# Dealing the second batch's selective scan out between the stages ahead of the first attention scores

## Chip, cores and metric

The kernel runs on one NeuronCore of a Trainium2 chip. The metric is device microseconds of that core for one launch; the figure for the kernel before is the median of 3 runs, 2120.05 us (2119.4 to 2121.59). A NeuronCore has TensorE (PE; its weight loads are shown apart as PEld), VectorE (DVE), ScalarE (ACT), GpSimd (POOL) and SyncE (SP), which issues the DMAs of this kernel.

## What is computed

The input x has 4 batches of 512 rows and 512 columns. Each batch goes through four residual blocks; each adds tanh of a gate times the block's result.

```
x += tanh(g0) * scan(ctx, z = layernorm(x))        # selective scan, 512 channels, 16 states
x += tanh(g1) * glu(layernorm(x))                  # ternary weights, 8-bit activations, 512 -> 2048 -> 512
x += tanh(g2) * attention(layernorm(x), ctx)       # 16 heads of 128, RMS-normed q and k
x += tanh(g3) * experts(layernorm(x))              # row t uses expert t % 4
scan: state = state * exp(delta * A) + (delta * u) * B ;  y = sum over 16 states of state * C
      y = (y + D * u) * silu(z)
glu:  out = bitlinear(silu(bitlinear(x, gate)) * bitlinear(x, val), out)
```

The batches are independent of one another; within a batch each block needs the one before it. The weights are scaled and split into float16 pairs (high and low part), so that three float16 matmuls stand for one of float32.

## The kernel before, in words

**Scan** (`scan(b)`, a generator). Four pieces of input projection and convolution (L507 to L523), four of softplus (L538 to L553), and then, twice over two channel tiles (`G=2`), 16 pieces, one for each state n, and four pieces that gate and add the result to x. A piece of a state loads two broadcast rows `bc` and `cc` (L590, L592), and for each of two channel tiles computes `dA` = exp on ACT (L596), `h` = du * bc on POOL (L186), the recurrence on DVE (L603, or L606 for 2 of 8), the product with `cc` on DVE (L604) or POOL, and four transposing matmuls that add the result up in PSUM (`py`, L579). A scan of this form is 48 pieces.

**GLU** (`bitnet(b)`, a generator of 24 pieces). Four row tiles; for each, the quantised rows (L669, L671), a DMA transpose (L673), four column blocks of gate and value matmuls (`pg` L687, `pv` L698) with their DVE steps (L692, L708, L710, L711), and the output projection (`po`, L733), whose operand passes through another DMA transpose (L731).

**Attention** goes head by head, in three phases that are one head apart: queries, scores with softmax, weighted sum. The main loop (from L1215) steps through 64 heads; in each it makes ten moves, and after each move it takes one piece of whatever stands in the list `behind`. Into that list go the scan and GLU of the next batch: batch 1 is entered 12 heads ahead of its own first head (`LEADS`), batches 2 and 3 16 heads ahead. So the second batch's scan and GLU lie beside heads of the first batch's attention. Keys of each group of four heads are made in some moves of the loop as well.

**Prologue.** Ahead of the main loop stand, in program order: the first batch's scan with the ternary weights between its pieces (L1173), the second batch's context (L1181), the first batch's GLU (L1182), the scaling and splitting ("staging") of the attention weights of head group 0 (L1183), the keys of group 0 (L1187), and the values of all four groups, 16 chunks that are stored to DRAM (`first_values`, L1188). Groups 1 and 2 are staged at iterations -1 and 1 of the main loop with large tiles (`STAGE`), group 3 from iteration 3 in small pieces (`staging_small`) that are taken two at a time after a softmax (`FILL0`, `filler`).

**Who decides the order.** The program's calls give priorities; a list scheduler in the build then decides the order in which instructions stand on each engine, and which buffer of a pool a tile gets. Work that is ready can therefore move ahead of its place in the program. On each engine, the SP queue too, instructions then start in that fixed order.

**Shared tiles.** The pool `mid` has six buffers of tag `g` and six of tag `v`. The scan's `bc` and `cc` and the GLU's hidden blocks `g` all take tag `g`; the scan's `h` and the GLU's `gv` take tag `v`. The four hidden blocks of a row tile stay in their buffers until that row tile is projected.[...]

Of the kernel before, what the change touches and what calls it, by code (L numbers as in the profile page):

```python
# [29 lines left out]
F32 = mybir.dt.float32  # L30
F16 = mybir.dt.float16
# [9 lines left out]
P = 128  # L41
# [23 lines left out]


MIDS = {"g": 6, "v": 6, "t": 4, "q": 2, "n": 1, "x": 1, "y": 2}
STAGE = (-1, 1)
STAGE_SMALL = {3: 3}
FILL0 = 2  # L70
RATE_S = 1.0
RATE_B = 1.0
SRB = 1
SHB = 1
EARLY = 1
SIDE0 = 5
SIDE1 = 1
SIDEN = 16
# [30 lines left out]
LO_POOL = {(b, h, 1) for b in range(3) for h in range(9, 16)}  # L109
HL = 2  # L110
PRE = 1
LEADS = {1: 12, 2: 16, 3: 16}
LEAD_B = 6


# [1 line left out]
def flamingo_kernel(  # L117
# [19 lines left out]
    def psum(pool, name, tag="m", bufs=None):  # L137
        if tag == "a":
            role = name.rstrip("_0123456789")
            tag = ATAG.get(role, "m")  # L140
            bufs = ABUF[tag]
        kw = {} if bufs is None else {"bufs": bufs}
        return pool.tile([P, 512], F32, tag=tag, name=name, **kw)

    def ap(name):
        return psum(psa, name, "a")
# [3 lines left out]
    def bigt(shape, dtype, name):  # L150
        return big.tile(shape, dtype, tag="big", name=name)
# [58 lines left out]
    def pow2(sq, name, pool=const, tag=None, bufs=1):  # L210
# [10 lines left out]
        nc.vector.reciprocal(S[:, 1:2], S[:, 0:1])  # L221
        return S

    def total_pow2(tot, pool, name):

        n = tot.shape[1]
        ps = ap(f"frobps{name}") if pool is None else psum(pool, f"frobps{name}")
        nc.tensor.matmul(ps[:, :n], ones, tot, start=True, stop=True)
        if n == 1:
            return pow2(ps[:, 0:1], name)  # L230
        s = sm(1, "ftot", f"ftot{name}")
        nc.vector.tensor_reduce(s, ps[:, :n], AX.X, ALU.add)
        return pow2(s, name)

    def frobenius(w, junk, pool, name):

        tot = sm(1, "frob", f"frob{name}")
        nc.scalar.activation(junk, w, AF.Square, accum_out=tot)
        return total_pow2(tot, pool, name)
# [16 lines left out]
    wq_d, wk_d, wo_d = [], [], []  # L256
    Sq, Sk, Sv, So, ceq = [], [], [], [], []

    def raw_load(name, src):
        raw = bigt([P, src.shape[1] * src.shape[2]], F32, f"raw{name}")  # L260
        with tc.issue_after(pin[0]) if pin[0] and PINS else nullcontext():
            nc.sync.dma_start(raw.rearrange("p (a b) -> p a b", a=src.shape[1]), src)
        return raw
# [3 lines left out]
    def run(steps):  # L267
        while True:
            try:
                next(steps)  # L270
            except StopIteration as e:
                return e.value

    def staging(name, src, n, ps_pool, raw=None, store=True):

        if raw is None:
            raw = raw_load(name, src)
        w = raw.shape[1]
        hl = bigt([P, 2 * w], F16, f"hl{name}")
        v = hl.rearrange("p (n s m) -> p n s m", n=n, s=2)  # L280
        pieces = [
            (raw[:, j * 512 : (j + 1) * 512], *(v[:, j, s] if n > 1 else v[:, 0, s, j * 512 : (j + 1) * 512] for s in range(2)))
            for j in range(w // 512)
        ]
        tot = sm(4, "stot", f"stot{name}", 2)
        for j, (r, hi, lo) in enumerate(pieces):
            nc.scalar.activation(hi, r, AF.Square, accum_out=tot[:, j : j + 1])
            yield
        S = total_pow2(tot[:, : len(pieces)], ps_pool, name)
        for r, hi, lo in pieces:  # L290
            split(r, hi, lo, S[:, 1:2])
            yield
        if not store:
            return None, S, hl
        d = dram.tile([P, 2 * w], F16, name=f"d{name}")
        nc.sync.dma_start(d, hl)
        return d, S, hl
# [29 lines left out]
            yield  # L327
        return d, S, None

    def stage_attention_weights(hg, ps_pool):  # L330
        run(attention_weights(hg, ps_pool, staging))

    def attention_weights(hg, ps_pool, staging):
        cols = slice(hg * 512, (hg + 1) * 512)
        d, S, _ = yield from staging(f"wq{hg}", Wq[hg], HG, ps_pool)
# [26 lines left out]

    def first_values(pool, ps_tile):

        for hg in range(NG):
            raw = pool.tile([P, 2, 512], F32, tag="rv", name=f"rawv{hg}", bufs=2)
            nc.sync.dma_start(raw, Wv[:, hg * 512 : (hg + 1) * 512].rearrange("(k p) c -> p k c", p=P))
            wv = pool.tile([P, 2, 2, 512], F16, tag="wv", name=f"wv{hg}", bufs=2)
            S = frobenius(raw, wv[:, 0], psv, f"wv{hg}")
            split(raw, wv[:, 0], wv[:, 1], S[:, 1:2])  # L370
            Sv.append(S)
            wv_d.append(dram.tile([P, 2048], F16, name=f"dwv{hg}"))
            nc.sync.dma_start(wv_d[hg], wv.rearrange("p s k c -> p (s k c)"))
            for b in range(PRE):
                for c, v in enumerate(
                    values_of(b, hg, wv, ps_tile, lambda s, d, n: pool.tile(s, d, tag="v", name=f"o{n}", bufs=VB))
                ):
                    nc.sync.dma_start(v_d[b][hg][:, c, :], v.rearrange("p s c -> p (s c)"))


    gamma_w = const.tile([P, 3], F32, name="gamma_w")
# [65 lines left out]
    raw = bigt([P, 2, T * P], F32, "inpraw")  # L447
# [203 lines left out]
        nc.vector.tensor_scalar(dn, m, 1.0 / (127.0 * gain), None, ALU.mult)  # L651
        return up, dn

    def bitnet(b, w_tile=bigt, ps_tile=lambda name: psum(pss, name), biases=None):
        xt = x_sb[b]
        w3 = []
        for i in range(3):
# [20 lines left out]
        def hidden(t, xqT, sgv):  # L678

            nm = f"{b}{t}"  # L680
            hs = []
            mx = sm(4, "hmx", f"hmx{nm}")
            for n in range(4):
                cols = slice(n * 512, (n + 1) * 512)
                pg = psum(pss, f"pg{nm}{n}")
                for k in range(T):
                    nc.tensor.matmul(pg, xqT[:, k, :], wg[:, k, cols], start=k == 0, stop=k == T - 1)  # L687
                g = midt([P, 512], F32, f"g{nm}{n}", "g")
                if biases is None:
                    nc.sync.dma_start(g, gate_b[cols].partition_broadcast(P))  # L690
                gb = g if biases is None else biases[0][:, cols]
                nc.vector.scalar_tensor_tensor(g, pg, sgv[:, 0:1], gb, ALU.mult, ALU.add)  # L692

                th = pg
                nc.scalar.activation(th, g, AF.Tanh, scale=0.5)
                pv = ps_tile(f"pv{nm}{n}")
                for k in range(T):
                    nc.tensor.matmul(pv, xqT[:, k, :], wv[:, k, cols], start=k == 0, stop=k == T - 1)  # L698
                v = midt([P, 512], F32, f"gv{nm}{n}", "v")
                if biases is None:  # L700
                    nc.sync.dma_start(v, val_b[cols].partition_broadcast(P))
                vb = v if biases is None else biases[1][:, cols]
                if (b, n) in GVP:
                    v2 = midt([P, 512], F32, f"gv2{nm}{n}", "t")
                    nc.scalar.activation(v2, pv, AF.Copy, scale=sgv[:, 1:2])
                    nc.gpsimd.tensor_tensor(v, v2, vb, ALU.add)
                else:
                    nc.vector.scalar_tensor_tensor(v, pv, sgv[:, 1:2], vb, ALU.mult, ALU.add)  # L708
                pool_mult(g, g, v)
                nc.vector.scalar_tensor_tensor(g, th, 1.0, g, ALU.add, ALU.mult)  # L710
                nc.vector.tensor_reduce(mx[:, n : n + 1], g, AX.X, ALU.max, apply_absolute_value=True)  # L711
                hs.append(g)
                yield

            return hs, mx
# [413 lines left out]
    def filler(ins):  # L1129

        for _ in range(FILL if atts[B - 1] else FILL0):
            with tc.issue_after(ins):
                while fill and next(fill[0], fill) is fill:
                    fill.pop(0)

    ak = ctx.enter_context(tc.tile_pool(name="ak", bufs=1))
    with tc.tile_pool(name="pro", bufs=1) as pro, tc.tile_pool(name="psp", bufs=4, space=PSUM) as psp:

        psv = pss
# [39 lines left out]
            biases.append(wide([P, HID], F32, f"bias{name}"))  # L1179
            nc.sync.dma_start(biases[-1], bias.partition_broadcast(P))  # L1180
        context(1, wide, junk, psv)  # L1181
        run(bitnet(0, wide, lambda name: psum(psp, name, "n", 2), biases))  # L1182
        for hg in range(EARLY):  # L1183
            stage_attention_weights(hg, psv)
        atts[0] = step, keys = attention(0)
        steps[0] = step
        run(keys(0, lambda name: psum(psp, name, "m", 2)))  # L1187
        first_values(pro, lambda name: psum(psp, name, "m", 2))  # L1188
    psa = ctx.enter_context(tc.tile_pool(name="psa", bufs=4, space=PSUM))
    at_pool = ctx.enter_context(ExitStack())  # L1190
    at = at_pool.enter_context(tc.tile_pool(name="at", bufs=1))
# [6 lines left out]
            for t in range(T)  # L1198
        ]

    in_bitnet = [False]
    behind, rate = [], 0.0

    def layer0(b):

        in_bitnet[0] = False
        if b >= 2:
            context(b, bigt, bigt, pss)
        yield from scan(b)
        in_bitnet[0] = True  # L1210
        yield from bitnet(b)


    n = B * NH
    for i in range(-2, n):  # L1215
# [34 lines left out]
                        next(keygen, None)  # L1250
        if i in STAGE_SMALL:
            fill.append(attention_weights(STAGE_SMALL[i], None, staging_small))
        if i in STAGE:
            for hg, j in enumerate(STAGE):
                if j == i:
                    stage_attention_weights(hg + EARLY, pss)
        if i >= 0 and i % NH == NH - 1:
            finish(i // NH)
        if i == n - NH + STAGE_E:
# [73 lines left out]
```

## Time and profile before

| What | Value |
|---|---|
| median of 3 runs | 2120.05 us |
| the profiled execution's own time | 2116.47 us |
| its span, first to last instruction | 2114.7 us |
| mean granted TensorE clock | 0.864 |
| PE busy | 1619.9 us (77%) |
| DVE busy | 1659.6 us (78%) |
| ACT busy | 1202.2 us (57%) |
| POOL busy | 1006.5 us (48%) |

The page puts busy time against the span, splits the span into 40 slices, and lists the costliest groups of instructions with the idle time before them. Stage times below are taken from the trace: the first batch's scan writes `py` until 179 us; its GLU runs its matmuls from 203 to 294 us; the keys of group 0 are made from 289 to 305 us; the values of the first batch from 306 to 358 us; the first query matmul starts at 376.5 us; the second batch's scan writes `py` from 430 to 634 us and its GLU's matmuls run from 658 to 765 us. A window of the trace gives, for each engine, busy microseconds and number of instructions in a stretch of time, then the granted TensorE clock, the DMA engines' busy share and what they moved.

### The profile page before, as it was taken

To read this page: it belongs to the slowest core of one execution; us is meant where nothing else is said; L and a number is where in the kernel's file an instruction comes from. 1 tells how busy PE (TensorE), PEld (TensorE's weight loads), DVE (VectorE), ACT (ScalarE), POOL (GpSimd) and SP (SyncE) were. 2 spreads that over 40 slices of the span, in tenths; PEclk is the share of its full clock that TensorE was granted. 3 is DMA by queue.
4 is the path that set the end of the run, shared out by engine and by line. 5 is a ranking of instruction groups with operands and counts; after the bars stand their busy time and mean duration, and the time that the engine had idled before them with its cause. 6 is when DMAs were issued, how large, how long until landed. Compare 5 with 4: busy or idle time off the path is not lost. (4 is left out here: it accounts for less than half of the span.)

```text
span 2114.7 us, 26915 instructions
## 1 busy us (share of the span) xinstructions
PE 1619.9 (77%) x8238; PEld 905.6 (43%) x8238; DVE 1659.6 (78%) x3237; ACT 1202.2 (57%) x2575; POOL 1006.5 (48%) x914
## 2 busy tenths in 40 slices
PE   3464654777676988777898967787899879788986
PEld 1343221345443444454444434444444445445445
DVE  5798855699998987999998679998885665555753
ACT  6866355665544666564546664654465565657633
POOL 2775330276664545766536367774253431313211
PEclk8555867889888998888899988898999989899998
DMA  7454176667888866776776567767765776867753
GB/s 248 157 166 139 25 194 224 191 157 200 188 223 209 191 138 159 191 179 164 184 184 143 121 152 206 176 165 192 165 148 124 169 165 189 182 163 192 184 127 100
DMA packets 525202, 358.08 MB, mean 169 GB/s; under 512 B 424768, under 2 KB 427456, under 8 KB 519040
## 3 DMA queue, kind: packets, MB, share of 16 engines
q1 hardware_dynamic: 525056, 356.36, 66.9%
q8 instruction: 64, 1.05, 0.2%
q14 instruction: 82, 0.67, 0.1%
HBM read 214.98 MB, written 38.54 MB: 120 GB/s over the span
## 5 line engine op out<-in xcount | busy, mean ns | idle before, releaser
L186 POOL TENSOR_TENSOR h<-du,bc 128x512 f32<-128x512 f32 x256 | 333.5, 1322 | 88.1 <-PE py L579 69.5
L579 PE MATMUL py<-ident,h 128*128 128x128 f32 x1024 | 196.8, 339 | 118.8 <-DVE h L604 109.1
L596 ACT ACTIVATE dA<-delta,A 128x512 f32<-128x512 f32 x256 | 172.0, 687 | 191.5 <-DVE h L604 132.1
L902 ACT ACTIVATE pr<-ps,nmx,rqs 128x512 f32<-128x512 f32 x256 | 196.9, 774 | 124.2 <-DVE nmx L894 119.4
L603 DVE TENSOR_TENSOR_SCAN dA<-dA,h 128x512 f32<-128x512 f32 x208 | 249.3, 1216 | 11.6 <-ACT dA L596 11.3
L252 PE MATMUL ps<-kT,qT 128*128 128x512 f16 x768 | 214.4, 402 | 49.8 <-ACT pr L902 45.4
L252 PE MATMUL pq<-axnT,wq 128*128 128x512 f16 x768 | 213.5, 436 | 35.2 <-DMA axnT<-xsa 15.0
L252 PE MATMUL pav<-pT,v 128*128 128x256 f16 x1536 | 205.7, 286 | 43.6 <-DVE v L244 14.7
L579 PEld LDWEIGHTS py<-ident,h 128*128 128x128 f32 x1024 | 163.0, 213 | 161.3 <-DVE h L604 139.5
L926 DVE SCALAR_TENSOR_TENSOR hl<-pr,den,hl 128x512 f16<-128x512 f32 x214 | 195.8, 926 | 24.7 <-POOL hl L925 15.0
L252 PEld LDWEIGHTS <-v 128*128 128x128 f16 x1536 | 156.2, 103 | 99.1 <-issue 30.8
L884 DVE TENSOR_REDUCE nmx<-ps 128x1 f32<-128x512 f32 x256 | 172.7, 680 | 28.6 <-PE ps L252 27.9
L252 PE MATMUL pwo<-wo,oT 128*128 128x512 f16 x768 | 180.9, 384 | 9.9 <-DVE oT L244 5.2
L252 PEld LDWEIGHTS <-cT 128*128 128x128 f16 x768 | 83.7, 110 | 170.1 <-issue 108.8
L925 POOL TENSOR_SCALAR hl<-pr,den 128x512 f16<-128x512 f32 x86 | 64.5, 750 | 189.1 <-DVE den L912 59.7
L252 PEld LDWEIGHTS <-wq 128*128 128x128 f16 x768 | 85.0, 112 | 154.4 <-issue 92.4
L252 PE MATMUL pk<-wk,cT 128*128 128x512 f16 x384 | 119.1, 457 | 33.9 <-DVE ssq L873 11.3
L186 POOL TENSOR_TENSOR g<-g,gv 128x512 f32<-128x512 f32 x64 | 83.5, 1310 | 120.3 <-DVE gv L708 44.6
L252 PEld LDWEIGHTS <-qT 128*128 128x128 f16 x768 | 77.9, 103 | 143.7 <-issue 77.5
L604 DVE TENSOR_TENSOR h<-dA,cc 128x512 f32<-128x512 f32 x208 | 138.0, 676 | 0.6
L183 POOL TENSOR_TENSOR rqs<-ssq,mhalf 128x4 f32<-128x4 f32 x64 | 69.0, 1078 | 134.9 <-DVE ssq L873 101.5
L252 PE MATMUL pw<-wv,cT 128*128 128x512 f16 x384 | 102.5, 413 | 28.7 <-DVE ov L244 11.9
(379 smaller groups left out, 3442.0 us busy)
## 6 DMA issues: line engine op xcount, KB each, us to landing
bc<-bd SPq DMA_DIRECT2D x112, 256.0 KB, 3.9
cc<-bd SPq DMA_DIRECT2D x112, 256.0 KB, 4.3
wq<-dwq SPq DMA_DIRECT2D x64, 256.0 KB, 3.6
wo<-dwo SPq DMA_DIRECT2D x64, 256.0 KB, 4.0
w<-w3d SPq DMA_DIRECT2D x12, 1024.0 KB, 7.0
g<-in_gate_b SPq DMA_DIRECT2D x48, 256.0 KB, 3.8
gv<-in_val_b SPq DMA_DIRECT2D x48, 256.0 KB, 4.4
de<-hle SPq DMA_DIRECT2D x9, 1024.0 KB, 5.3
```

What stands on the lines that cost most here:

```text
L183: nc.gpsimd.tensor_tensor(res, arg, mhalf[:, : arg.shape[1]], ALU.pow)
L186: nc.gpsimd.tensor_tensor(out, a, b, ALU.mult)
L252: nc.tensor.matmul(ps, l, r, start=first and i == 0, stop=last and i == n - 1)
L579: nc.tensor.matmul(ys[g // gs][:, g % gs, t, :], src[:, g::T], ident, is_transpose=True, start=first and t == 0 and g % gs == 0, stop=last ...
L596: last = nc.scalar.activation(dA, delta[:, t0 + t, :], AF.Exp, scale=A[:, t0 + t, n : n + 1])
L603: nc.vector.tensor_tensor_scan(dA, dA, h, 0.0, ALU.mult, ALU.add)
L604: nc.vector.tensor_tensor(h, dA, cc, ALU.mult)
L884: nc.vector.tensor_reduce(nmx[:, c : c + 1], ps, AX.X, ALU.max, negate=True)
L902: mark[0] = nc.scalar.activation(pr, scs[c], AF.Exp, bias=nmx[:, one], scale=rqs[:, one], accum_out=den[:, c - c0 : c - c0 + 1],).ins
L925: nc.gpsimd.tensor_scalar(hl[:, c, 0], prs[c], den[:, one], 1.0, ALU.mult, ALU.mult)
L926: nc.vector.scalar_tensor_tensor(hl[:, c, 1], prs[c], den[:, one], hl[:, c, 0], ALU.mult, ALU.subtract)
```

## The change

The second batch's scan and GLU are entered into `behind` in the prologue, directly after its context, and its entry in `LEADS` goes. A new function `beside` runs a stage and, after each of its pieces, takes as many pieces from `behind` as a rate says: 1 beside the first GLU (24 pieces), 0.5 beside the staging of weights (20 pieces for each group), 1 beside the first keys (4), 0.5 beside the first values (16). That makes 24 + 20 + 4 + 8 = 56 pieces: the whole scan (48) and 8 of 24 pieces of the GLU; the main loop takes the other 16 from its first move on.

Group 1 is staged in the prologue as well (`EARLY = 2`); group 2 moves from large tiles to `staging_small`, entered at iteration -1, and three of its pieces are taken after a softmax rather than two (`FILL0 = 3`). The staging in the prologue takes tiles of the prologue's own pool (`wide`, five buffers, which also hold the GLU's weights and biases) in place of the `big` pool, whose buffers the scan needs. The first GLU's gate matmuls write two banks of `psp` in place of the four of `pss`, which the scan takes over.

```
-STAGE = (-1, 1)
-STAGE_SMALL = {3: 3}
-FILL0 = 2
+STAGE_SMALL = {-1: 2, 3: 3}
+FILL0 = 3
...
-EARLY = 1
+EARLY = 2
...
-LEADS = {1: 12, 2: 16, 3: 16}
+LEADS = {2: 16, 3: 16}
+BESIDE = (1.0, 0.5, 1.0, 0.5)
...
+    def pool_tag(pool):
+        return ("m", None) if pool is pss else ("n", 2)
...
-        ps = ap(f"frobps{name}") if pool is None else psum(pool, f"frobps{name}")
+        ps = ap(f"frobps{name}") if pool is None else psum(pool, f"frobps{name}", *pool_tag(pool))
...
-    def staging(name, src, n, ps_pool, raw=None, store=True):
+    def staging(name, src, n, ps_pool, raw=None, store=True, tile=None):
+        tile = tile or bigt
...
-            S = frobenius(raw, wv[:, 0], psv, f"wv{hg}")
+            S = frobenius(raw, wv[:, 0], psp, f"wv{hg}")
...
                     nc.sync.dma_start(v_d[b][hg][:, c, :], v.rearrange("p s c -> p (s c)"))
+                    yield
...
-                pg = psum(pss, f"pg{nm}{n}")
+                pg = g_tile(f"pg{nm}{n}")
...
+    def layer0(b):
+        in_bitnet[0] = False
+        if b >= 2:
+            context(b, bigt, bigt, pss)
+        yield from scan(b)
+        in_bitnet[0] = True
+        yield from bitnet(b)
...
         context(1, wide, junk, psv)
-        run(bitnet(0, wide, lambda name: psum(psp, name, "n", 2), biases))
+        behind.append((1, layer0(1)))
+        def beside(steps, pieces):
+            rate = 0.0
+            for _ in steps:
+                rate += pieces
+                while rate >= 1:
+                    rate -= 1
+                    next(behind[0][1])
+        def narrow(name):
+            return psum(psp, name, "m", 2)
+        beside(bitnet(0, wide, lambda name: psum(psp, name, "n", 2), biases, narrow), BESIDE[0])
+        def staged(*args):
+            return staging(*args, tile=wide)
         for hg in range(EARLY):
-            stage_attention_weights(hg, psv)
+            beside(attention_weights(hg, psp, staged), BESIDE[1])
         atts[0] = step, keys = attention(0)
         steps[0] = step
-        run(keys(0, lambda name: psum(psp, name, "m", 2)))
-        first_values(pro, lambda name: psum(psp, name, "m", 2))
+        beside(keys(0, narrow), BESIDE[2])
+        beside(first_values(pro, narrow), BESIDE[3])
...
-        if i in STAGE:
-            for hg, j in enumerate(STAGE):
-                if j == i:
-                    stage_attention_weights(hg + EARLY, pss)
```

More of the change, by code (lines that the diff above doesn't have):

```diff
@@ L257, in flamingo_kernel, with raw_load @@
     Sq, Sk, Sv, So, ceq = [], [], [], [], []
-    def raw_load(name, src):
-        raw = bigt([P, src.shape[1] * src.shape[2]], F32, f"raw{name}")
+    def raw_load(name, src, tile=bigt):
+        raw = tile([P, src.shape[1] * src.shape[2]], F32, f"raw{name}")
         with tc.issue_after(pin[0]) if pin[0] and PINS else nullcontext():
@@ L272, in run @@
                 return e.value
-    def staging(name, src, n, ps_pool, raw=None, store=True):
+    def staging(name, src, n, ps_pool, raw=None, store=True, tile=None):
+        tile = tile or bigt
         if raw is None:
-            raw = raw_load(name, src)
+            raw = raw_load(name, src, tile)
         w = raw.shape[1]
-        hl = bigt([P, 2 * w], F16, f"hl{name}")
+        hl = tile([P, 2 * w], F16, f"hl{name}")
         v = hl.rearrange("p (n s m) -> p n s m", n=n, s=2)
@@ L328, in staging_small @@
         return d, S, None
-    def stage_attention_weights(hg, ps_pool):
-        run(attention_weights(hg, ps_pool, staging))
     def attention_weights(hg, ps_pool, staging):
@@ L652, in scales, with bitnet @@
         return up, dn
-    def bitnet(b, w_tile=bigt, ps_tile=lambda name: psum(pss, name), biases=None):
+    def bitnet(b, w_tile=bigt, ps_tile=lambda name: psum(pss, name), biases=None, g_tile=lambda name: psum(pss, name)):
         xt = x_sb[b]
@@ L1134, in filler @@
                     fill.pop(0)
+    in_bitnet = [False]
+    behind = []
+    def layer0(b):
[5 more added lines that the diff above has]
+        yield from bitnet(b)
     ak = ctx.enter_context(tc.tile_pool(name="ak", bufs=1))
@@ L1199, in finish @@
         ]
[L1201 to L1211, printed above, removed]
+    rate = 0.0
     n = B * NH
```

## Prediction

> **What bounds the kernel now.** I read the page first, then busy time by stage, then the waits of VectorE (DVE), then the rows of the scan. On the page DVE (78%) and TensorE (77%) are level, so neither average decides; the stages do. Each line below is a stretch of time with its length, then busy us (number of instructions) of PE, PEld, DVE, ACT and POOL, the granted clock, the DMA share and GB/s.
>
> ```profile
> 194.00:272.00 78.00, 48.28 (x175) 19.13 (x175) 67.40 (x165) 30.33 (x50) 29.16 (x27) 0.74 0.28 69
> 272.00:304.00 32.00, 17.25 (x50) 6.78 (x51) 17.89 (x50) 20.52 (x60) 9.93 (x11) 0.61 0.82 253
> 304.00:382.00 78.00, 39.68 (x127) 15.35 (x125) 31.25 (x81) 33.64 (x71) 11.46 (x14) 0.71 0.74 228
> 382.00:440.00 58.00, 46.68 (x215) 22.95 (x215) 47.04 (x88) 45.55 (x98) 22.29 (x21) 0.93 0.68 161
> 440.00:640.00 200.00, 146.06 (x766) 93.06 (x767) 193.41 (x291) 105.18 (x229) 135.84 (x113) 0.85 0.78 195
> 640.00:800.00 160.00, 134.44 (x655) 67.94 (x654) 139.88 (x320) 97.31 (x227) 81.98 (x78) 0.92 0.75 170
> 800.00:1160.00 360.00, 297.14 (x1510) 169.77 (x1509) 330.39 (x619) 203.86 (x449) 219.18 (x195) 0.90 0.72 175
> 1579.00:1697.00 118.00, 103.18 (x552) 54.48 (x550) 74.25 (x164) 65.92 (x168) 49.79 (x53) 0.99 0.68 147
> ```
>
> From 440 to 640 us the second batch's scan runs beside attention and DVE is busy 97% of the time. Staging, keys and values (272 to 382 us) use DVE for only 49 of 110 us; they wait on short chains, as the waits of DVE from 194 to 381 us show (total us, times, longest):
>
> ```profile
> DVE ftotwo L232 <- PE frobpswo L228: 12.5, 2, 9.5
> DVE ov L244 <- ACT ov L243: 11.8, 8, 2.3
> ```
>
> The last window is the third batch's attention with neither a scan nor a GLU beside it: PE 87% busy at a clock of 0.99, 6.65 heads in 118 us, 17.7 us a head. So there is idle DVE in the prologue; but a scan taken away from attention leaves heads that TensorE bounds, and their DVE idles in turn.
>
> **The change, part by part.** The built order of the changed kernel shows what moves; durations are those of this profile. The scan's rows:
>
> ```profile
> L186 POOL TENSOR_TENSOR h<-du,bc 128x512 f32<-128x512 f32 x256 | 333.5, 1322 | 88.1 <-PE py L579 69.5
> L603 DVE TENSOR_TENSOR_SCAN dA<-dA,h 128x512 f32<-128x512 f32 x208 | 249.3, 1216 | 11.6 <-ACT dA L596 11.3
> L604 DVE TENSOR_TENSOR h<-dA,cc 128x512 f32<-128x512 f32 x208 | 138.0, 676 | 0.6
> ...
> bc<-bd SPq DMA_DIRECT2D x112, 256.0 KB, 3.9
> ```
>
> One scan of this form has 48 x 1.216 (L603) + 48 x 0.676 (L604) + 16 x 1.21 (L606) = 110 us of recurrence on DVE. Convolution, softplus, silu and gating add about 36 us, the GLU pieces that come along 35, and the staging of group 2, which goes, takes off 5. Up to the first query split the order holds 308 us of DVE durations from 194 us on, against 131 before: +177. Consecutive instructions overlap a little: before, 131 us of durations are 116.5 us of busy time, a factor of 0.89. POOL gains 132 us (80 products at 1.27 to 1.32, 9 of the GLU, du), ACT 76. All 64 recurrences stand ahead of the first query, so that the change would not do what it says is ruled out; the GLU's hidden half does too, its projections not yet.
>
> I time three stretches, between points where both orders can be compared.
>
> *First GLU to first query split* (before 194 to 382 us, 188 us):
> - Until the first recurrence: 61.5 us of durations, 54 busy. At the first window's 86% that is 62 us.
> - The first 13 state pieces with the rest of the first GLU: 78 us, 70 busy. `bc` and `cc` now share six `g` buffers with the GLU's hidden blocks, of which a row tile holds four. The buffer list has each of `bc` 5, 6 and 7 in the buffer of the one ahead, so a piece is a chain: 3.9 us from issue to landing, then two POOL products of 1.27, 6.4 us; 13 x 6.4 = 83 us. Against 70 busy, the chain decides: 83.
> - To the end of the recurrence, with the staging of groups 0 and 1 and keys beside it: 106 us of durations, 94 busy. All six buffers serve the scan. DMA: about 9 MB of `bc` and `cc`, 10 MB of staging, 3 MB of the rest; 22 MB at the 195 to 228 GB/s of the windows is 96 to 113 us. I take 105.
> - The rest (gating, GLU hidden blocks, 11 of 16 value chunks): 62 us of durations, 55 busy. Before, 16 chunks took 52 us (306 to 358), so 11 take 36, and 24 more pass until the query. I take 62.
>
> Sum 312, first query at 506 us: 124 later.
>
> *First query to the weighted sum of head 13* (before 382 to 791 us, 409 us): DVE durations fall from 415 to 272, 242 busy, so TensorE decides. A head alone costs 17.7 us, of which the values computed for later groups (48 matmuls at about 0.22 in the window, 10.5 us over 6.65 heads) are 1.6; batch 0 loads them, so 16.1. Lead-in to the first weighted sum 35 (before 42, with convolution in it), 13 heads 209, the rest of the second GLU about 30 of PE (`po` 17, half of `pg` and `pv` 17, a little of it in the lead-in), the third scan's opening, which the scheduler moves up from head 12 to head 10, about 20. Sum 294: 115 less.
>
> *From there to head 10 of batch 1* (before 791 to 1158 us, 367 us): the opening brought forward leaves 351 us of durations in place of 380. At the same busy share, 367 x 351 / 380 = 339; TensorE would allow 297 - 25 busy. I take 337: 30 less. From this point on the two orders have the same DVE work behind them, within 6 us, and stand alike, so I count nothing after it.
>
> Total +124 - 115 - 30 = -21. The profiled execution took 2116.5 us (span 2114.7 and 1.8 around it): 2095.5. The median of the runs lies 3.6 above it: 2099, taken as 2098.
>
> **What I cost at nothing, or from both sides.** *Two gate banks in place of four*: the first bank is held from 203.3 to 214 us; 16 blocks x 10.7 / 2 = 86 us, under the 145 us of the first two parts; without that cover up to 20 us. *Group 2 in small pieces*: ACT idled 16 us for the loads of group 3's 20 pieces; 20 more cost up to 16 us of ACT, which is busy under 60% in that stretch; zero to 16 if the softmax stands behind a load, and I take zero. Below zero it cannot be. *Raw weights in the GLU's five wide buffers*: the first raw load now stands behind the last row tile's hidden blocks; the scan's second half covers it. *SP queue*: `bc` and `cc` stand behind hqT transposes, which wait for DVE's quantised blocks; before, such a transpose takes about 3 us to the matmul. Zero to 13 x 1 us, in the range.
>
> [...] The staging's split reads two; the same instruction takes
>
> ```profile
> L244 DVE SCALAR_TENSOR_TENSOR hlwo<-rawwo,Swo,hlwo 128x512 f16<-128x512 f32 x8 | 5.6, 748 | 0.8 <-ACT hlwo L243 0.8
> ```
>
> 0.75 us in the prologue, with POOL quiet, and up to 1.84 (minimum/median/maximum in ns) while POOL forms the scan's products:
>
> ```profile
> L244 DVE SCALAR_TENSOR_TENSOR shlwk<-srawwk,Swk,shlwk x2: 727/1285/1843, 618.6 to 628.3; 128x512 f16<-128x512 f32 x2
> ```
>
> [...] By the rows the median excess is 0.13 to 0.54, so 20 x 0.3 = 6 us; that is inside the 105.
>
> [...] The rows have 0.85 beside the scan and 0.99 without it. [...] Of the price, slow matmuls in the prologue, the first scan (60 to 180 us, clock 0.50, DVE still busy 113 of 120 us) says it is hidden.
>
> **Rivals.**
> - *More than that*: the prologue runs DVE at the 94% of the first scan, 273 / 0.94 = 290, and the rest as above: -43, 2077. For it: 97% at 440 to 640. Against: the `g` buffers.
> - *No change*: the matmuls for values were not on the path of the heads alone, whose softmax chains then set the 17.7 us; 13 x 1.6 = 21 us eats the gain: 2120. For it: ACT waits for `nmx`, of up to 11 us, in the third batch's tail. Against: PE is busy 87% there.
> - *Slower*: the chain over the shared `g` buffers, in the 13 pieces beside the first GLU. At the landing of 4.1 to 4.6 us seen at 440 to 640, one more POOL product ahead (1.3), and the queue (0.4), a piece takes 8.9 us: 13 x 8.9 = 116 in place of 83, +33. That gives -21 + 33 = +12: 2132. It decides from 83 + 21 = 104 us, 8.0 us a piece. For it: in-order engines, so a late `bc` holds back the GLU's instructions behind its recurrence too. Against: DMA is idle 72% of the first GLU now.
>
> **Chances.** My case, 2076 to 2115: 0.47. Beyond it: 0.11. Within 0.2% (about what a measurement of this kernel can tell from no change; 2115.8 to 2124.3): 0.11. Slower: 0.31. So faster 0.58. The range reaches down to the first rival with the third stretch at 97% of DVE too (312 / 0.97 = 322, 15 less; 2062, of which I keep 2066) and up to the slower rival with half of the ACT cost (2132 + 8): 2066 to 2140.
>
> **What would show it.** Right: DVE over 85% busy from 194 us to the first query at about 506; 16 to 18 us a head, clock over 0.95, in batch 0's heads 3 to 9; head 10 of batch 1 about 21 us earlier, and the same distance to the end. Wrong: waits of POOL `h` for `bc` beside the first GLU; recurrences over 8 us a piece apart there; heads near 20 us in batch 0; or a change in distance after head 10 of batch 1.

## The result, and the profile after

The changed kernel takes 2219.18 us (median of 4 runs, 2216.27 to 2223.52) against 2119.73 us for the kernel before (4 runs): the ratio is 1.0471, 95% interval 1.0442 to 1.0501. It is 99 us slower, outside the range of the prediction and on the other side of no change. The profiled execution took 2223.52 us, its span is 2221.7 us and its mean clock 0.851. Lines after the edits are shifted by about 3: L603 is now L606, L604 is L607, L579 is L582, L317 is L321.

The page of the kernel after, with the lines that answer to those of before:

```profile
span 2221.7 us, 27012 instructions
...
PE 1644.1 (74%) x8238; PEld 916.1 (41%) x8238; DVE 1665.0 (75%) x3237; ACT 1204.2 (54%) x2575; POOL 1002.2 (45%) x914
...
L186 POOL TENSOR_TENSOR h<-du,bc 128x512 f32<-128x512 f32 x256 | 332.8, 1317 | 107.4 <-PE py L582 61.9
L606 DVE TENSOR_TENSOR_SCAN dA<-dA,h 128x512 f32<-128x512 f32 x208 | 250.2, 1219 | 10.8 <-ACT dA L599 8.1
L607 DVE TENSOR_TENSOR h<-dA,cc 128x512 f32<-128x512 f32 x208 | 138.7, 680 | 2.9 <-DMA cc<-bd 1.9
```

PE, DVE, ACT and POOL have as many instructions as before. Of busy time PE has 24 us more (0.1996 us a matmul against 0.1966, see below), DVE 5 more, ACT 2 more, POOL 4 less. The scan's rows on DVE and POOL keep their old mean durations to within 1%. So most of the 107 us more of span are waiting. The windows of the kernel after say where (columns as in the prediction: length, busy PE, PEld, DVE, ACT, POOL, clock, DMA share, GB/s). The first three lines are stretch 1 in the prediction's own parts, the fourth is stretch 2, the fifth six heads inside it, from head 3 to head 9, the last stretch 3:

```profile
194.00:263.00 69.00, 46.75 (x147) 17.69 (x148) 58.21 (x122) 36.42 (x57) 26.01 (x21) 0.77 0.34 92
263.00:446.00 183.00, 101.84 (x420) 61.89 (x419) 174.68 (x277) 95.10 (x193) 129.54 (x106) 0.70 0.65 188
446.00:520.00 74.00, 46.70 (x189) 21.66 (x190) 50.52 (x123) 28.02 (x45) 24.47 (x23) 0.82 0.77 222
520.00:905.00 385.00, 270.72 (x1260) 141.02 (x1257) 227.34 (x495) 197.04 (x475) 132.68 (x128) 0.81 0.63 148
654.00:808.00 154.00, 102.79 (x483) 54.20 (x481) 72.07 (x175) 67.87 (x181) 38.05 (x40) 0.80 0.63 151
905.00:1268.00 363.00, 292.31 (x1478) 165.12 (x1479) 318.35 (x603) 185.05 (x423) 197.86 (x180) 0.89 0.69 164
```

The kernel before in the same two stretches, from its first query to head 13 and on to head 10 of batch 1:

```profile
382.00:791.00 409.00, 318.28 (x1610) 180.05 (x1611) 372.63 (x684) 243.44 (x545) 235.49 (x207) 0.89 0.76 182
791.00:1158.00 367.00, 304.05 (x1520) 172.38 (x1519) 336.09 (x631) 206.79 (x455) 222.34 (x198) 0.89 0.71 173
```

In stretch 2 DVE lost 145 us of busy time and PE 48, yet the stretch lost only 24 us. The busiest engine there, TensorE, is at 70%, and a head takes 154 / 6 = 25.7 us. The scan was moved as intended; the room that it left was not used. The ledger, in us of the profiled spans (the edges of the windows are rounded to whole us, so a window can be 1 us off its entry); e1 is the first experiment below:

| Stretch | before | predicted | after | e1 |
|---|---|---|---|---|
| 1: to the first query | 188 | 312 | 326 | 330 |
| 2: to head 13 | 409 | 294 | 385 | 286 |
| 3: to head 10 of batch 1 | 367 | 337 | 363 | 367 |
| from there to the end | 957 | 957 | 953 | 951 |

The prediction missed the span by 128 us, 91 of them in stretch 2. What stands there is shown by the waits of the kernel after from 590 to 780 us (total us, times, longest):

```profile
PE frobpswk L231 <- ACT shlwk L321: 39.7, 2, 20.0
...
PE frobpswo L231 <- ACT shlwo L321: 20.1, 2, 10.4
ACT shlwo L321 <- DMA srawwo<-in_Wo: 19.9, 7, 3.9
ACT shlwo L246 <- DMA srawwo<-in_Wo: 18.5, 6, 4.7
```

`sraw` and `shl` are the small staging pieces of head groups 2 and 3. TensorE's longest waits are ahead of the staging's tiny matmul `frobps` (at most four columns), which adds up the squares; that waits for ACT, and ACT waits for loads. The timeline of ACT and PE shows how the pieces do it (start, duration, instruction, in brackets the idle time before it and what ended it):

```profile
629.74 0.71 ACT L926 ACTIVATE hl<-pr,den 128x512 f16<-128x512 f32 x1
634.38 0.63 ACT L321 ACTIVATE shlwo<-srawwo 128x512 f16<-128x512 f32 x1 [3.94 <-DMA srawwo<-in_Wo]
...
638.04 0.63 ACT L321 ACTIVATE shlwo<-srawwo 128x512 f16<-128x512 f32 x1 [2.93 <-DMA srawwo<-in_Wo]
...
641.61 0.63 ACT L321 ACTIVATE shlwo<-srawwo 128x512 f16<-128x512 f32 x1 [2.85 <-DMA srawwo<-in_Wo]
...
642.38 0.59 PE L231 MATMUL frobpswo<-stotwo,ones 128*128 128x4 f32 x2 [9.72 <-ACT shlwo L321]
...
642.83 1.85 PE L871 MATMUL psq<-ones,sq 128*128 128x1 f32 x8
...
646.70 0.78 ACT L905 ACTIVATE pr<-ps,nmx,rqs 128x512 f32<-128x512 f32 x1 [0.89 <-DVE nmx L897]
```

Between the `hl` at 629.7 and the next exp (`pr`) at 646.7 us stand 17 us, and the three piece instructions shown take 1.9 of them. Each waits for its own load, since there is one `sraw` buffer and the next load is issued only when the piece has left it (the second piece ends at 638.76 us, the SP queue issues the next load at 638.78). The exp behind them is held up twice. It stands behind the pieces in ACT's order; and what it waits for last, `nmx`, needs `psq`, the squared length of the queries, which stands behind `frobps` in TensorE's order. The input of `psq` was ready at 626.6 us; it starts at 642.8, after `frobps` has waited 9.7 us for ACT's pieces.

The code behind it is unchanged by the edit; with `SRB = 1` the load of piece j + 1 follows the work on piece j:

```
    def staging_small(name, src, n, ps_pool):
...
            raw = at.tile([P, 512], F32, tag="sraw", name=f"sraw{name}{j}", bufs=SRB)
...
        for j in range(2 * k):
            hl = at.tile([P, 2, 512], F16, tag="shl", name=f"shl{name}{j}", bufs=SHB)
...
            if j + SRB < 2 * k:
                raws.append(load(j + SRB))
            yield
```

### The profile page after: what moved, and what is told of

It reads as the page before. It is cut to its first block, busy times and chain, and to the rows that moved or that the text cites. A ratio compares the mean times of both kernels' runs of the same rounds, so it can differ in the third digit from the quotient of the medians.

```text
span 2221.7 us, 27012 instructions
## 1 busy us (share of the span) xinstructions
PE 1644.1 (74%) x8238; PEld 916.1 (41%) x8238; DVE 1665.0 (75%) x3237; ACT 1204.2 (54%) x2575; POOL 1002.2 (45%) x914
## 5 line engine op out<-in xcount | busy, mean ns | idle before, releaser
L582 PE MATMUL py<-ident,h 128*128 128x128 f32 x1024 | 203.5, 349 | 142.7 <-DVE h L607 125.6
L606 DVE TENSOR_TENSOR_SCAN dA<-dA,h 128x512 f32<-128x512 f32 x208 | 250.2, 1219 | 10.8 <-ACT dA L599 8.1
L255 PE MATMUL pq<-axnT,wq 128*128 128x512 f16 x768 | 222.5, 450 | 43.2 <-DMA wq<-dwq 14.2
L582 PEld LDWEIGHTS py<-ident,h 128*128 128x128 f32 x1024 | 168.1, 214 | 186.3 <-DVE h L607 160.4
L607 DVE TENSOR_TENSOR h<-dA,cc 128x512 f32<-128x512 f32 x208 | 138.7, 680 | 2.9 <-DMA cc<-bd 1.9
L255 PEld LDWEIGHTS <-oT 128*128 128x128 f16 x768 | 75.0, 99 | 107.1 <-issue 13.9
```

What stands on the lines that cost most here:

```text
L255: nc.tensor.matmul(ps, l, r, start=first and i == 0, stop=last and i == n - 1)
L582: nc.tensor.matmul(ys[g // gs][:, g % gs, t, :], src[:, g::T], ident, is_transpose=True, start=first and t == 0 and g % gs == 0, stop=last ...
L606: nc.vector.tensor_tensor_scan(dA, dA, h, 0.0, ALU.mult, ALU.add)
L607: nc.vector.tensor_tensor(h, dA, cc, ALU.mult)
```

## Experiments

Theory A: the lost time in stretch 2 is the small pieces, each waiting for its load ahead of the softmax on ACT. Theory B: heads without a scan are long by themselves, the dealt-out scan and the reordered GLU leave a chain that the prediction did not see. Theory C: the longer prologue is the loss. All ratios are against the kernel before on the same chip, with 95% intervals; "span" is that of the profiled execution.

### e1: without the small pieces

```
-            fill.append(attention_weights(STAGE_SMALL[i], None, staging_small))
+            for of in (wq_d, wk_d, wo_d, Sq, Sk, So, ceq):
+                of.append(of[1])
```

> The changed kernel without the 40 small staging pieces of groups 2 and 3: their heads take the scaled weights of group 1, so this part of the computation is left out. Theory A (the small pieces, each waiting on ACT for a load into one single raw buffer, hold back the softmax of the first batch): the 386 us from the first query to the weighted sum of head 13 fall to about 295 to 315, heads 3 to 9 to 16 to 18 us each, total 2115 to 2150. Theory B (heads without a scan are slow by themselves, by the clock or the softmax chain): heads stay at 22 us and more, total 2190 to 2215. Theory C (the longer prologue is the loss): the stretch falls, but the total stays above 2190.

Measured: 2127.57 us, ratio 1.0028 (1.0010 to 1.0046), span 2129.0. Windows of e1: stretch 2, from head 3 to head 9, stretch 3.

```profile
524.00:811.00 287.00, 245.59 (x1237) 129.06 (x1236) 207.07 (x428) 165.91 (x402) 119.37 (x117) 0.92 0.64 141
622.00:717.00 95.00, 83.51 (x468) 46.02 (x466) 61.20 (x131) 51.69 (x147) 34.37 (x36) 1.00 0.67 149
811.00:1178.00 367.00, 291.78 (x1490) 164.40 (x1489) 316.55 (x611) 191.19 (x438) 205.56 (x187) 0.90 0.70 165
```

Six heads that took 154 us take 95, 15.9 us each before rounding, and PE is 88% busy in them at a clock of 1.00 instead of 0.80. The 40 pieces cost 92 us of median time (2219.18 - 2127.57), nearly all of the loss. That the pieces are the loss holds; B falls for stretch 2, and C falls, since the total drops with a first stretch as long as before. That the pieces' waits are it, and not their work, e1 cannot tell; e4 can. It also leaves e1 without the gain that was forecast; that is the second question.

### e4: four loads ahead, two results

```
-SRB = 1
-SHB = 1
+SRB = 4
+SHB = 2
...
-            raw = at.tile([P, 512], F32, tag="sraw", name=f"sraw{name}{j}", bufs=SRB)
+            raw = midt([P, 512], F32, f"sraw{name}{j}", "v")
```

> The changed kernel with the raw tiles of the small pieces taken from the six buffers of tag v, four loads ahead in place of one, and two result tiles in place of one. All the work stays. Theory A: ACT's waits for these loads (85 us over 40 pieces) nearly vanish and 60 to 90 us come back: 2130 to 2160. Theory B: within 10 us of 2219. Theory C: within 15 us of 2219.

Measured: 2142.59 us, ratio 1.0090 (1.0069 to 1.0110), span 2138.4. All 40 pieces are there, in the same numbers after each softmax. Windows of e4, stretch 2 and from head 3 to head 9:

```profile
520.00:827.00 307.00, 256.24 (x1262) 135.36 (x1260) 228.45 (x492) 191.47 (x465) 125.40 (x122) 0.89 0.78 184
629.00:737.00 108.00, 92.48 (x481) 50.62 (x479) 74.13 (x176) 70.17 (x187) 39.55 (x42) 0.92 0.87 206
```

With the same work (within 10 instructions on each engine) and only the buffers changed, stretch 2 falls from 385 to 307 us. Of the pieces' 92 us, 77 were the single buffers and 15 remain. ACT no longer waits for any `sraw` load; its idle time just ahead of the small pieces falls from 94 to 19 us, as much as the kernel gains. TensorE's longest wait for `frobps` falls from 20.0 to 5.4 us:

```profile
PE frobpswk L231 <- ACT shlwk L321: 9.5, 2, 5.4
```

### e10: one result buffer, three buffers for queries

```
-MIDS = {"g": 6, "v": 6, "t": 4, "q": 2, "n": 1, "x": 1, "y": 2}
+MIDS = {"g": 6, "v": 6, "t": 4, "q": 3, "n": 1, "x": 1, "y": 2}
...
-SRB = 1
+SRB = 4
...
-            raw = at.tile([P, 512], F32, tag="sraw", name=f"sraw{name}{j}", bufs=SRB)
+            raw = midt([P, 512], F32, f"sraw{name}{j}", "v")
```

> The changed kernel with four raw loads ahead, one result tile, and three buffers of tag q in place of two. Before the first query DVE stood 10 us behind a q buffer that a DMA transpose of the attention's input still read. If that buffer is what the tail of the prologue waits for, the stretch to the first query split falls from 326 to 312 to 318 us and the total from 2143 to about 2130; if the SP queue's order is, it stays at 323 to 328.

Measured: 2153.30 us, ratio 1.0166 (1.0123 to 1.0210); stretch 1 327 us, stretch 2 327. The expected total was 2143 us or less, a miss. Two readings. Stretch 2 is 20 us longer than in e4, and ACT idles 53 us ahead of the pieces against 19; 42 of the 53 end with the store of the result tile, as here in stretch 2:

```profile
ACT shlwo L246 <- DMA dwo<-shlwo: 17.5, 4, 7.3
```

So the single result tile is a wait of its own. (The third `q` buffer differs from e4 too; none of these waits names it.) And the tail of stretch 1 is not held by the two `q` buffers, since it is 327 us with three and 326 in the kernel after.

### e2 and e5: fewer small pieces, more staging in the prologue

e2 stages all four groups in the prologue with large tiles, e5 three of them and the fourth in small pieces, one after a softmax:

```
e2:
-STAGE_SMALL = {-1: 2, 3: 3}
-EARLY = 2
-BESIDE = (1.0, 0.5, 1.0, 0.5)
+STAGE_SMALL = {}
+EARLY = 4
+BESIDE = (1.0, 0.25, 1.0, 0.5)
e5:
-STAGE_SMALL = {-1: 2, 3: 3}
-FILL0 = 3
-EARLY = 2
-BESIDE = (1.0, 0.5, 1.0, 0.5)
+STAGE_SMALL = {-1: 3}
+FILL0 = 1
+EARLY = 3
+BESIDE = (1.0, 0.35, 1.0, 0.5)
```

> The changed kernel with all four groups staged in the prologue in large tiles, at a rate of 0.25 scan pieces per staging piece, and no small pieces. Theory A: heads 3 to 9 at 16 to 18 us as in the run without small pieces; the prologue grows by 20 splits on DVE (15 us) and up to 10 MB of transfers (45 us, part of it hidden), so total 2140 to 2170. Theory B: heads as slow as in the changed kernel, total 2240 or more. Theory C: total above 2219, since the prologue grows.

> The changed kernel with group 2 staged in the prologue and only group 3 in small pieces, one piece after a softmax in place of three, entered at iteration -1; still one single raw buffer. On ACT one small piece then stands between two softmax steps, where the changed kernel has up to five in a row. Theory A, in the form that it is the row of pieces that has to wait for loads one after another: with half the pieces and about 8 us between two of them the loads land in time, ACT's wait for them falls from 85 us to under 20 and heads 3 to 9 take 17 to 19 us; the prologue grows by about 20 us for group 2; total 2150 to 2165. If instead each piece costs its load whatever stands between, 20 pieces at about 4 us make heads 3 to 9 take 20 us or more: total 2180 to 2200.

Measured: e2 2170.82 us, 1 us above what was expected, ratio 1.0230 (1.0196 to 1.0265), stretches 372, 297, 357. e5 2153.72 us, ratio 1.0167 (1.0135 to 1.0200), stretches 343, 296, 364. Against e1, e2 pays 42 us in stretch 1 for two more groups in large tiles, e5 pays 13 there for one, and 10 in stretch 2 for twenty pieces taken singly. So staging has a price in the prologue too, up to 21 us a group; and twenty pieces taken singly, even with one buffer, have a small one: ACT waits 16 us for their loads, 0.8 us for each, against 2.1 in the kernel after. That agrees with waits that add up where pieces stand in a row, but e5 changes the number and the place of the pieces too.

### e7 and e8: two pieces after a softmax; half of the dealing

e7 is e4 with `FILL0 = 2`. e8 is e7 with the scan dealt out at half the rates:

```
e8:
-FILL0 = 3
-BESIDE = (1.0, 0.5, 1.0, 0.5)
+FILL0 = 2
+BESIDE = (0.5, 0.25, 1.0, 0.25)
```

> The changed kernel with four raw loads ahead (as in the run with four) and two pieces after a softmax in place of three. Theory A: the rest of the waiting in a row of pieces shrinks; the stretch from first query to head 13 falls from 307 to 290 to 300 us: 2125 to 2140. If the three at a time mattered by themselves apart from loads: the same.

> As the run before in this list (four loads ahead, two pieces), with half the rates of scan pieces beside the first GLU and the values (0.5, 0.25, 1, 0.25): 30 pieces in the prologue, 18 of the scan and the whole GLU in the main loop. If the balance of DVE between the two stretches decides, the prologue falls by 60 to 80 us and the heads grow by 40 to 70: 2100 to 2125, below both kernels at best. If work moved early and work moved late cost the same, no change from the run before: 2125 to 2140.

Measured: e7 2158.23 us, ratio 1.0186 (1.0154 to 1.0217), stretches 324, 314, 369, a miss: it is 16 us slower than e4, and why stays open. e8 2133.35 us, ratio 1.0079 (1.0044 to 1.0113), stretches 288, 349, 352. From e7 to e8 stretch 1 becomes 36 us shorter and stretch 2 35 us longer. Between these two stretches the moved work is paid for almost one for one: stretch 1 is itself filled by it (DVE busy 89% of stretch 1 in e1, 292.29 of 330 us). Yet e8 is 25 us faster than e7 in all, from a stretch 3 that is 17 us shorter and 9 us behind it; why is open. It is a miss too: 2100 to 2125 us were expected if the balance of DVE decides, and no change from e7 if not.

### e12: the kernel before, without its twenty small pieces

```
-            fill.append(attention_weights(STAGE_SMALL[i], None, staging_small))
+            for of in (wq_d, wk_d, wo_d, Sq, Sk, So, ceq):
+                of.append(of[2])
```

> The kernel before without its 20 small staging pieces: group 3's heads take the scaled weights of group 2, so this part of the computation is left out. Set against the changed kernel without small pieces (2128) it gives the price of moving the scan alone. Theory A: the 20 pieces cost the kernel before 5 to 20 us, total 2100 to 2115; moving the scan then costs 13 to 28 us by itself. If the pieces cost nothing beside a scan: 2117 to 2122.

Measured: 2115.32 us, ratio 0.9990 (0.9970 to 1.0011), stretches 188, 380, 395, 959. Twenty pieces in their old place cost nothing that can be told: stretch 2 gains 29 us and stretch 3 gives 28 back. Set beside e1 it also prices the rest of the change, with no small pieces in either: 1.0028 - 0.9990 = 0.0038 of 2120 us, 8 us slower (2 to 14 from the two intervals), where the prediction had 21 us faster. The spans give the same sign: stretch 1 +142, stretch 2 -93, stretch 3 -28, the rest -7 (2129.0 - 2115.5 = 13.5). The comparison is kind to the change: e1 stages two groups in all and e12 three (27 fewer instructions on DVE and 30 on ACT in e1), so it does not price the dealing of the scan by itself.

### e3, e6 and e11: small pieces in the kernel before

```
e3:
-STAGE = (-1, 1)
-STAGE_SMALL = {3: 3}
-FILL0 = 2
+STAGE = (-1,)
+STAGE_SMALL = {-1: 2, 3: 3}
+FILL0 = 3
e6 (its raw tiles from tag "v", as in e4):
-SRB = 1
-SHB = 1
+SRB = 4
+SHB = 2
e11 (e6, and):
-STAGE_SMALL = {3: 3}
-FILL0 = 2
+STAGE_SMALL = {-1: 3}
+FILL0 = 1
```

> The kernel before, with group 2 staged in small pieces at iteration -1 and three pieces after a softmax, as in the change, and nothing else changed. Theory A: beside the scan DVE bounds the heads and part of ACT's waiting is hidden; 20 more pieces at about 2 us each cost 0 to 40 us: 2120 to 2160. Theories B and C: no change beyond 10 us, 2115 to 2130.

> The kernel before with the raw tiles of group 3's small pieces from the six buffers of tag v, four loads ahead, and two result tiles. Theory A: ACT waited 16 us for these loads, beside a scan that bounds DVE: 0 to 15 us faster, 2105 to 2120. Against it: tag v is the scan's, whose products then have fewer buffers: up to 15 us slower, 2135.

> The kernel before with four raw loads ahead for the small pieces (tag v), two result tiles, and group 3's pieces one after a softmax from iteration -1 on in place of two from iteration 3. Theory A: loads have landed and no softmax stands behind two pieces; 0 to 10 us under the run with four loads ahead: 2100 to 2112. If pieces in the first heads cost more than in later ones: 2115 or more.

Measured: e3 2202.84 us, ratio 1.0377 (1.0355 to 1.0399), stretches 193, 476, 370. This was a miss, outside what any of the theories expected. Forty small pieces in place of twenty, taken earlier and by threes, cost 81 us (2202.84 against 2121.63) in a kernel whose heads do have the scan beside them. So the scan's cover would not have saved the prediction's zero. But the waits for loads explain only a part of it: ACT waits 43 us for them in e3, 16 in the kernel before. Head 3 ends at 564 us instead of 489, and by then ACT has waited only 12 us for small loads, while 53 of the scan's recurrences have started, against 18 in the kernel before. The built order has let the scan run on ahead of the heads; how much of the 81 us that costs is open.

e6 2109.66 us, ratio 0.9958 (0.9935 to 0.9981): the kernel before with deeper buffers for its twenty pieces, and faster than both kernels. Stretch 2 is 403 us against 409, the heads of it 32.6 us against 34.2, ACT's idle time ahead of the pieces 14.1 us against 21.5. Since leaving the pieces out altogether gained nothing that can be told (e12), it is not shown that these waits are what e6 gained.

e11 2161.25 us, ratio 1.0210 (1.0160 to 1.0259), stretches 185, 430, 384, a miss. With deep buffers and one piece at a time it is still slower by 52 us than e6. Its second scan begins at 492 us instead of 441; the early entry of the pieces moved other work in the built order, and which of it matters is open.

### e9: the third scan's products from DVE to POOL

```
-        yield from scan(b)
+        yield from scan(b, (0, 2, 4) if b == 2 else DVE_OF_8)
```

> The kernel before; in the third batch's scan 3 of 8 products with cc stay on DVE in place of 6, the rest go to POOL: 24 products of 0.68 us leave DVE (16 us), 32 us come to POOL. The question is what sets the stretch from head 13 of batch 0 to head 10 of batch 1 (367 us before, 363 in the changed kernel in spite of 20 us less DVE work). If DVE sets it, it falls to 350 to 355 and the total to 2100 to 2110. If the heads' own chain and TensorE set it, it stays within 5 us of 367 or grows with POOL: 2115 to 2135.

Measured: 2126.50 us, ratio 1.0031 (1.0003 to 1.0059). Its stretch 3:

```profile
793.00:1171.00 378.00, 300.39 (x1506) 168.76 (x1505) 333.64 (x595) 203.24 (x449) 252.33 (x219) 0.87 0.69 167
```

DVE has 36 instructions fewer than before (595 against 631) and the stretch is 11 us longer. POOL has 30 us more, and DVE's busy time fell by only 2.5 us, so this is weak proof; but it gives no sign that a stretch with less for DVE becomes shorter.

## Why the prediction was wrong

**The step that failed** is "Group 2 in small pieces", a cost put at nothing: "20 more cost up to 16 us of ACT, which is busy under 60% in that stretch; zero to 16 if the softmax stands behind a load, and I take zero". Measured: the forty pieces cost 92 us (e1), of which 77 go with buffers alone (e4 against after). Four things in that step were wrong:

- The row was scaled by the count of pieces: 16 us of load waits for 20 pieces in the profile before, 0.8 us each. In the profile after it is 85 us of load waits for 40, 2.1 us each. The diff also raises the number taken after a softmax from 2 to 3, and with one buffer each piece behind the first waits for a load of its own. That this number sets the wait per piece is argued: one at a time gave 0.8 us (e5), but three at a time in the kernel before gave only 1.1 (e3).
- ACT at under 60% busy was read as reserve. In stretch 2 of the kernel after it is busy 51% (197.04 of 385 us), and its waits cost all the same: behind the load stood the exp of the next head, and the squares that TensorE's `frobps` waits for.
- The cost was put on ACT alone. TensorE has its own place in the chain, the `frobps` matmul in its fixed order, with the heads' own `psq` behind it: 60 us of its waits from 590 to 780 us are there (39.7 + 20.1).
- TensorE's clock fell with the waits. From head 3 to head 9 it is 0.80, against 1.00 in e1; a matmul there is 102.79 / 483 = 0.213 us busy against 83.51 / 468 = 0.178, so up to 17 of the 59 us that six heads lost are slower matmuls, 483 x 0.035. Over stretch 2 a matmul is 270.72 / 1260 = 0.215 us busy at a clock of 0.81, and in e4 256.24 / 1262 = 0.203 us at 0.89. The longest wait of TensorE for `frobps` in that stretch is 20.0 us in the kernel after and 5.4 in e4; e1 has none and a clock of 0.92. The prediction's windows have the clock at 0.85 beside the scan and 0.99 without it, and it named slow matmuls as a price in the prologue, hidden there (0.50 in the first scan), but not as a price of new waits in the heads. That the waits bring the clock down is read from these three runs; how they do it is not shown.

The bound "zero to 16" came from a row with another place and another number in a row. Two whole loads per three pieces, at the 3.1 us from issue to landing that a load of `sraw` for Wo takes in the median of the profile after, would be 40 x 2/3 x 3.1 = 83 us. This estimate comes close to the 85 us here; for e3, with the same pieces and one buffer, it is nearly twice the 43 us that ACT waited, so it is no rule.

**Heads alone**: right, as e1 shows without the pieces. 16.1 us was forecast and 15.9 measured, stretch 2 at 286 us against 294. So the rival "no change", that softmax chains set the heads' 17.7 us, is refuted.

**Stretch 1**: right up to the end of the recurrence, short in its tail, and DVE is 87% busy in it (58.21 + 174.68 + 50.52 of 326 us), as the signs had it. To the first recurrence 69 us against 62, to the end of the recurrence 183 against 83 + 105 = 188, the tail 74 against 62. The chain of `bc` over shared `g` buffers, on which the slower rival rested, did not decide: the first 13 pieces are 5.9 us apart (recurrences from 262.6 to 339.5 us), under the 6.4 of the chain, and this is all that POOL waited for `bc` from 263 to 350 us:

```profile
POOL h L186 <- DMA bc<-bd: 16.5, 9, 3.8
```

In the tail two single waits, from the waits of the kernel after from 446 to 520 us, are as large as the 12 us that were missed there:

```profile
PE pq L255 <- DMA wq<-dwq: 14.2, 1, 14.2
...
DVE hq L732 <- DMA axnT<-xsa: 10.1, 1, 10.1
```

Both are DMAs of the SP queue. A third `q` buffer did not shorten it (e10, which still waits 6.2 us for `axnT`); that the queue's order is the cause is argued, not shown.

**The splits beside the scan**: right. The three rows of large splits, each with two tensors read (`raw` and `hl`), have 20 instructions from 263 to 446 us and 9.4 + 8.0 + 3.4 = 20.8 us:

```profile
L247 DVE SCALAR_TENSOR_TENSOR hlwq<-rawwq,Swq,hlwq 128x512 f16<-128x512 f32 x8 | 9.4, 1205 | 0.0
L247 DVE SCALAR_TENSOR_TENSOR hlwo<-rawwo,Swo,hlwo 128x512 f16<-128x512 f32 x8 | 8.0, 1024 | 0.0
L247 DVE SCALAR_TENSOR_TENSOR hlwk<-rawwk,Swk,hlwk 128x512 f16<-128x512 f32 x4 | 3.4, 859 | 0.0
```

At 0.75 us they would take 15.0, so the excess is 5.8 us against the 6 that were taken.

**Stretch 3**: wrong, 30 us short. "At the same busy share, 367 x 351 / 380": DVE's durations did fall, from 382 to 361 us (351 was counted), but the stretch stayed at 363 to 367 us in after and e1, and DVE's busy share fell instead, from 0.92 to 0.88 (0.86 in e1). DVE at 92% was a sign of the stretch, not its bound; PE lost 12 us of busy time there as well. What sets its length stays open; e9 gives only that fewer DVE instructions were no help.

**After head 10 of batch 1**: right, 953 against 957 us.

So, of the -21 us, three terms: the pieces, +92; stretch 1 without them, +18 (330 against 312); stretch 3, +30; with -8 for stretch 2 and -6 for the rest. Without the pieces the change is still 6 us slower than the kernel before (e1), 8 us if their twenty are left out of that one too (e12), and not 21 faster. The prediction's list of signs named the right one: "heads near 20 us in batch 0"; they came at 25.7.

## What to carry to other kernels

Before work that waits for a load is put between the steps of a loop whose steps wait for one another, count its buffers and how many pieces stand in a row. With one buffer a piece cost ACT 2.1 us of waiting for its load here (85 us for 40 pieces), with ACT 51% busy in the stretch, and TensorE waited up to 20.0 us for the result. Do not price it from the idle time of a row in another place, and give it the loads ahead first; here deeper buffers alone took back 77 of 92 us (e4). Moving work out of a busy stage into one with idle time gained nothing here: stretch 1 grew by 142 us for 122 that went out of the two stretches behind (e1 against e12).

## What the runs showed of the hardware

Two waits of TensorE of about 20 us and two of about 10 went with a mean clock of 0.73 to 0.74 over the 190 us in which they lie (590 to 780 us in the profile after), while six heads without them hold 1.00 (e1, 95 us). A 256 KB load that is issued in turn with the work on it comes to 3.1 us from issue to landing in the median (2.5 to 5.8, 16 loads of `srawwo` in the profile after); in the three instructions shown above ACT sees 2.9 to 3.9 us of it as idle time.
